# Smaller array tiles for score and pointwise products in a four-layer attention and convolution kernel

## The chip, the cores and the metric

One core of a Trainium2 chip runs the whole kernel. The time is device time in microseconds of one execution; a version is measured in several executions and the median is taken. TensorE multiplies matrices in an array of 128 rows by 128 columns. A product whose contraction has 64 or fewer elements, or whose result has 64 or fewer rows, can be put in a part of the array (a tile), and products in different tiles can run beside one another. A "64x128 tile" here has 64 rows (contraction) and 128 columns (rows of the result). Each f32 product appears in the profile as two matmul instructions, each with its own weight load, so the counts in the profile are twice those in the code.

## The reference

The input is a tensor `x` of 4 images, 64 by 64 positions, 64 channels, f32. Four layers follow one another:

```
layer 0   q, k, v = x Wq + bq, x Wk + bk, x Wv + bv     (per image, 4096 tokens of 64 channels)
          a = softmax(q k^T) over the keys;  out[n] = sum over queries m of a[m, n] v[m];  x = gamma * out + x
layer 1   y = layernorm(x); y = pointwise 64->256; depthwise 3x3; y = y1 * y2
          y = y * channel_weights(mean(y)); x = x + beta * pointwise 128->64 (y)
          z = layernorm(x); z = pointwise 64->256; z = z1 * z2; x = x + gamma * pointwise 128->64 (z)
layer 2   scores between the 64x64 positions of one map (softmax attention over 4096 entries); x = x + result
layer 3   theta, phi, g = x theta_W, x phi_W, x g_W      (64 -> 32 channels)
          y = softmax(theta phi^T) g; wy = y w_W + w_b; wy normalised over the batch; x = x + wy
```

In layer 2 the reference reads the tensor with its axes as (B, C, H, W), so that it too is attention of 4096 entries by 4096, with a contraction of 64. Layers 0, 2 and 3 each hold two large products per image: the scores (4096 x 4096 results) and the products of the exponentials with the values.

## The kernel before

The fast path keeps all four images in SBUF in the tile `X`, channels in partitions: partitions 0 to 63 hold one half of an image's tokens, 64 to 127 the other half. A second, general path runs only if a check of ranges at the end asks for it; it does not run on these inputs, and the change does not touch it.

PSUM is cut into two pools. `new_ps` gives one of three slots `ps` of 128 partitions by 1024 f32 (two banks each, so each half of 512 columns is one bank), `new_acc` one of two slots `acc` of 128 by 512. The exponentials go to six buffers `e` of 128 by 2048 in SBUF.

The order of the work is written out by hand for TensorE, ScalarE and VectorE (`manual_schedule`). `items` is a list of score steps, 32 per image for layers 0 and 2 and 64 per image for layer 3, each with an estimate of its length. `run` walks the list: it issues the score step of item i, lets two lanes (`conv` for layer 1, `misc` for projections, loads and closings) issue what has come due by the estimated clock, then issues what `due[i]` holds, above all the products of an earlier item, and lets the lanes run again. The order is fixed when the program is built and does not depend on measured times. The sequence of layers is: layer 0 of the four images, with layer 1 of each image threaded through layer 0 of the next; layer 2 of image 0, with layer 1 of the last image (and the end of that of image 2) threaded through; then layer 2 of image 1, layer 3 of image 0, layer 2 of image 2, layer 3 of image 1, layer 2 of image 3, layer 3 of images 2 and 3.

The places that matter here:

- Layer 0 scores, L1008: item t computes 128 columns of scores against all 4096 tokens as four `ps` slots (g = 0 to 3). In a slot, r = 0, 1 picks the row half of the array and the bank of the slot; both products use the same 128 columns of `m.q` as weights in 64x128 tiles. ScalarE takes the exponential of each slot (L1012). The products of earlier items, L1032, use the whole 128 rows and 64 columns: 128x64 tiles.
- Query projection, L975: the same form as a score slot, with the weights `wq`, before VectorE adds the bias (L979).
- Layer 1 pointwise products from 64 to 256 channels, L1103 and L1160: per image 8 tiles of `ps` each, 64x128, then a copy by ScalarE (L1108, L1165) or VectorE (L1167).
- Layer 2 scores, L1207, and products, L1224: both in 64x64 tiles already, four to a `ps` slot (`quads`), and not changed.
- Layer 3 scores, L1321: item n takes two `ps` slots at once; four products of contraction 32, one for each group of 32 rows (k = 0 to 3), 32x128 tiles. Slot k // 2, half k % 2. ScalarE then takes the two exponentials (L1326). The products, L1348, are in 128x32 tiles; a sum of the exponentials is made by VectorE (L1344) or, one item in ten, by TensorE (L1337).

A score step starts when its `ps` slot has been read by the exponential that used it last; a product step starts when the exponentials of its item are there.

Of the kernel before, what the change touches and what calls it, by code (L numbers as in the profile page):

```python
# [691 lines left out]
def fast_path(ctx: ExitStack, tc: tile.TileContext, a: dict, out: bass.AP, bad):  # L692
# [36 lines left out]
    mm = nc.tensor.matmul  # L729
# [236 lines left out]
    def project0(b):  # L966
        x, m = X[:, b], im[b]
        m.q, yv = new_big("q"), new_big("yv")
        m.y = yv[:, 0:2048]
        m.v = yv[:, 2048:4096].rearrange("p (t c) -> p t c", c=C)  # L970
        for j, w in ((0, "q"), (0, "v"), (1, "q"), (2, "q"), (1, "v"), (3, "q")):
            ps = new_ps()
            if w == "q":
                for s in range(2):
                    mm(  # L975
                        ps[:, bass.ts(s, 512)], wq[64 * s : 64 * s + 64, :], tok(x, s, j),
                        start=True, stop=True,
                    )
                nc.vector.tensor_scalar_add(  # L979
                    m.q[:, 0:N].rearrange("p (s n) -> p s n", s=2)[:, :, bass.ts(j, 512)],  # L980
                    ps.rearrange("p (s n) -> p s n", s=2), bqk,
                )
            else:
                for i in range(8):
                    mm(ps[:, bass.ts(i, 128)], x[:, bass.ts(8 * j + i, 128)], wv, start=True, stop=True)  # L985
                for s in range(2):
                    nc.vector.tensor_add(
                        m.v[:, 16 * s + 8 * j : 16 * s + 8 * j + 8, :],
                        ps.rearrange("p (t s c) -> p t s c", s=2, c=C)[:, :, s, :],
                        bv.unsqueeze(1).to_broadcast([128, 8, C]),  # L990
                    )
            yield 3.4
# [3 lines left out]
    def layer0(b):  # L996
        x, m, first = X[:, b], im[b], len(items)
        tiles = {}

        def scores(t):  # L1000
            es = [new_e() for _ in range(2)]
            zs = sm.tile([128, 4], F32, tag="zs", name="zs", bufs=4)
            vq = sm.tile([128, C], F32, tag="vq", name="vq", bufs=4)
            for g in range(4):
                ps = new_ps()
                for r in range(2):
                    rows_ = slice(64 * r, 64 * r + 64)
                    mm(  # L1008
                        ps[:, bass.ts(r, 512)], m.q[rows_, bass.ts(t, 128)],
                        x[rows_, bass.ts(g, 512)], start=True, stop=True,  # L1010
                    )
                act(  # L1012
                    es[g // 2][:, bass.ts(g % 2, 1024)], ps, AF.Exp, bias=SHIFT0,
                    accum_out=zs[:, g : g + 1],
                )
            tiles[t] = es, vq, zs

        def scale(t):
            es, vq, zs = tiles[t]
            tot = sums0[:, b, t : t + 1]  # L1020
            nc.vector.tensor_reduce(tot, zs, AX.X, ALU.add)
            rec = sm.tile([128, 1], F32, tag="rec", name="rec")
            nc.vector.reciprocal(rec, tot)
            nc.vector.tensor_scalar_mul(vq, m.v[:, t, :], rec)

        def products(p, half):
            accs = [new_acc() for _ in range(2)]
            for t in (2 * p, 2 * p + 1):
                es, vq, _ = tiles[t]
                for g in range(2):  # L1030
                    for r in range(2):
                        mm(  # L1032
                            accs[g][64 * r : 64 * r + 64, :], vq,
                            es[half][:, 1024 * g + 512 * r : 1024 * g + 512 * r + 512],
                            start=t == 2 * p, stop=t == 2 * p + 1,
                        )
            for g in range(2):
                cols = bass.ts(2 * half + g, 512)
                stt(  # L1039
                    (x if p == 15 else m.y)[:, cols], accs[g], gam0,  # L1040
                    (m.y if p else x)[:, cols], ALU.mult, ALU.add,
                )

        for t in range(32):
            items.append((lambda t=t: scores(t), 3.6))
        for p in range(16):
            for half in range(2):
                at(first + 2 * p + 2 + half, lambda p=p, half=half: products(p, half))
        for t in range(32):
            at(first + t, lambda t=t: scale(t))  # L1050
# [34 lines left out]

    def layer1(b):
        x = X[:, b]
        y = xn.tile([128, 2048], F32, tag="xn", name="xn")
        yield from norm(x, y)
        yg = new_big("yg")[:, 0:N].rearrange("p (w h) -> p w h", h=H)  # L1090
        ysum = sm.tile([128, 4], F32, tag="ysum", name="ysum")
        for r in (1, 0):
            pad = new_pad()
            nc.gpsimd.memset(pad[:, 0:PW], 0.0)
            nc.gpsimd.memset(pad[:, 65 * PW : 66 * PW + 2], 0.0)
            nc.gpsimd.memset(
                pad[:, PW : 65 * PW].rearrange("p (w h) -> p w h", h=PW)[:, :, 0:1], 0.0
            )
            inner = pad[:, PW + 1 : 65 * PW + 1].rearrange("c (p q s h) -> c q p s h", p=2, s=2, h=PW)
            for j in range(4):  # L1100
                ps = new_ps()
                for s in range(2):
                    mm(  # L1103
                        ps[:, bass.ts(s, 512)], pw1[64 * s : 64 * s + 64, bass.ts(r, 128)],
                        tok(y, s, j), start=True, stop=True,
                    )
                for s in range(2):
                    act(  # L1108
                        inner[:, bass.ts(j, 4), :, s, 0:H],
                        ps[:, bass.ts(s, 512)].rearrange("c (q p h) -> c q p h", p=2, h=H),  # L1110
                        AF.Identity, bias=pwb[:, 0, r : r + 1],
                    )
                yield 3.5
            for j in range(4):
                w0 = 16 * j
                y2 = yg[:, w0 : w0 + 16, :]
                out_ = y2 if r else new_t("y1").rearrange("p (w h) -> p w h", h=H)
                for k in range(9):
                    o = (w0 + k % 3) * PW + k // 3
                    win = pad[:, o : o + 16 * PW].rearrange("p (w h) -> p w h", h=PW)[:, :, 0:H]  # L1120
                    wt = V("L1_conv_dw_w", 2 * k + r)
                    if k == 0:
                        nc.vector.tensor_scalar(out_, win, wt, V("L1_conv_dw_b", r), ALU.mult, ALU.add)
                    else:
                        stt(out_, win, wt, out_, ALU.mult, ALU.add)  # L1125
                    yield 1.8
                if not r:
                    stt(y2, out_, 1.0, y2, ALU.mult, ALU.mult, accum_out=ysum[:, j : j + 1])
                    yield 1.8
# [3 lines left out]
        ps = new_ps()  # L1133
# [21 lines left out]
        for j in range(4):  # L1155
            t, u = new_t(), new_t("u")
            for r in range(2):
                ps = new_ps()
                for s in range(2):
                    mm(  # L1160
                        ps[:, bass.ts(s, 512)], pw3[64 * s : 64 * s + 64, bass.ts(r, 128)],
                        tok(z, s, j), start=True, stop=True,
                    )
                if r == 0:
                    act(t, ps, AF.Identity, bias=pwb[:, 1, 0:1])  # L1165
                else:
                    stt(u, ps, pwb[:, 1, 1:2], t, ALU.add, ALU.mult)  # L1167
                yield 3.5
            ps = new_ps()
            for s in range(2):  # L1170
                mm(ps[64 * s : 64 * s + 64, 0:512], pw4, u[:, bass.ts(s, 512)], start=True, stop=True)  # L1171
            act(t[:, 0:512], ps[:, 0:512], AF.Identity, bias=resb[:, 1:2], scale=V("L1_conv_gamma"))
            xs = x[:, bass.ts(j, 512)]
            nc.vector.tensor_add(xs, xs, t[:, 0:512])
            yield 3.5
# [135 lines left out]
    def layer3(b):  # L1311
# [3 lines left out]
        def scores(n):  # L1315
            nb, mc = n // 32, n % 32
            e = es[n] = new_e()
            tiles = [new_ps(), new_ps()]
            for k in range(4):
                rows_ = slice(32 * k, 32 * k + 32)  # L1320
                mm(  # L1321
                    tiles[k // 2][:, bass.ts(k % 2, 512)], m.ph[rows_, bass.ts(mc, 128)],
                    m.th[rows_, bass.ts(nb, 512)], start=True, stop=True,
                )
            for kp in range(2):
                act(e[:, bass.ts(kp, 1024)], tiles[kp], AF.Exp)  # L1326

# [272 lines left out]
```

## Time and profile before

| What | Value |
|---|---|
| Time, median of 3 runs | 2721.74 us (2719.4 to 2723.67) |
| Span of the profiled execution | 2718.6 us |
| Scores of layer 0, L1008, busy | 482.7 us, 2048 matmuls |
| Scores of layer 2, L1207, busy | 470.4 us, 4096 matmuls |
| Scores of layer 3, L1321, busy | 321.2 us, 2048 matmuls |
| Products of layers 0, 2, 3 (L1032, L1224, L1348), busy | 468.4, 468.0 and 272.0 us |
| Pointwise, L1103 and L1160, busy | 35.8 and 35.0 us, 128 matmuls each |
| Query projection, L975, busy | 17.1 us, 64 matmuls |
| Granted TensorE clock, mean | 0.994 |

The profile is of one execution. "PE" is TensorE's matmuls, "PEld" its weight loads, "ACT" ScalarE, "DVE" VectorE. A group is named by its line, then out<-in by tile names, rows*columns of the array, and the shape of the data that streams through it. The chain of waits is followed back from the last instruction; in order of time it lists start, length, engine, tile, line and how many instructions were merged in a piece. The length of a piece in it runs to the start of the next one, so waits inside it are part of it. In the timeline of one engine, what stands in brackets is the idle time before a piece and what ended it.

### The profile page before, as it was taken

Reading aid. Unit: us, or ns where it says so; the run is one execution under the profiler, and the core shown is the slowest. Engines: PE = TensorE matmul, PEld = TensorE weight load, DVE = VectorE, ACT = ScalarE, POOL = GpSimd, SP = SyncE. Lnnn points to the kernel's source line nnn. Section 1 sums busy time; section 2 is a strip of 40 time slices with the busy share of each in tenths; the row PEclk is TensorE's granted clock in tenths of the full one; section 3 lists DMA queues with packets and bytes.
Section 4 is the critical chain, followed back from the end, with each engine's and each line's share of the span. In section 5 each row is a group of like instructions: output and inputs, shape, how many; then the busy total and the mean of one; then the engine's idle time right before and its main releaser. Section 6 shows DMA issues by size and latency. Waiting matters only on the chain.

```text
span 2718.6 us, 41825 instructions
## 1 busy us (share of the span) xinstructions
PE 2656.8 (98%) x18042; PEld 902.6 (33%) x18042; DVE 1349.0 (50%) x1507; ACT 1724.6 (63%) x2796; POOL 16.6 (1%) x66
## 2 busy tenths in 40 slices
PE   8999999999999999999999999999999999999996
PEld 3343333333333333323333332243322333322222
DVE  3232478437773478216720027920058700088888
ACT  4545655565556555555655668855678756578886
POOL 2000000000000000000000000000000000000000
PEclk9999999999999999999999999999999999999998
DMA  3000000000000000000010000010000010010001
GB/s 71 0 1 1 1 1 1 1 1 1 1 1 1 8 8 1 1 1 17 1 32 1 16 1 1 1 32 1 17 1 1 1 32 1 1 32 1 1 1 64
DMA packets 17349, 24.33 MB, mean 9 GB/s; under 512 B 2460, under 2 KB 10885, under 8 KB 17157
## 3 DMA queue, kind: packets, MB, share of 16 engines
q1 hardware_dynamic: 16085, 20.47, 3.1%
q8 instruction: 143, 2.34, 0.4%
q0 software_dynamic: 672, 0.56, 0.1%
q10 hardware_dynamic: 400, 0.56, 0.1%
q14 instruction: 49, 0.40, 0.0%
HBM read 4.80 MB, written 4.19 MB: 3 GB/s over the span
## 4 chain that ended last, share of the span: by engine, by line
PE 94%; DVE 4%; ACT 2%; issue 0%; DMA 0%; ACTq 0%; DVEq 0%
PE acc L1032 17%; PE ps L1008 17%; PE acc L1224 16%; PE ps L1207 16%; PE ps L1321 11%; PE acc L1348 9%; PE ps L1103 1%; PE ps L1160 1%; PE accz L1337 1%; PE ps L1078 1%; PE ps L1143 1%; PE ps L1171 1%; PE ps L1064 1%; PE ps L1302 1%; PE ps L985 1%; DVE tg L1344 0%
## 5 line engine op out<-in xcount | busy, mean ns | idle before, releaser
L1012 ACT ACTIVATE e<-ps 128x1024 f32<-128x1024 f32 x512 | 517.1, 1024 | 343.4 <-PE ps L1008 231.0
L1215 ACT ACTIVATE e<-ps 128x1024 f32<-128x1024 f32 x512 | 517.1, 1024 | 308.1 <-PE ps L1207 308.0
L1326 ACT ACTIVATE e<-ps 128x1024 f32<-128x1024 f32 x512 | 495.4, 1022 | 94.9 <-PE ps L1321 85.1
L1344 DVE TENSOR_TENSOR tg<-tg,e 128x2048 f32<-128x2048 f32 x214 | 490.4, 2292 | 26.1 <-ACT e L1326 7.4
L1008 PE MATMUL ps<-X,q 64*128 64x512 f32 x2048 | 482.7, 608 | 11.3 <-ACT e L1012 4.2
L1207 PE MATMUL ps<-ko 64*64 64x512 f32 x4096 | 470.4, 593 | 7.8 <-ACT ko L1189 5.5
L1224 PE MATMUL acc<-e,X 64*64 64x512 f32 x4096 | 468.0, 591 | 2.7 <-DVE X L1039 2.1
L1032 PE MATMUL acc<-e,vq 128*64 128x512 f32 x2048 | 468.4, 599 | 0.0
L1321 PE MATMUL ps<-tg,ph 32*128 32x512 f32 x2048 | 321.2, 640 | 0.5 <-ACT e L1326 0.5
L1039 DVE SCALAR_TENSOR_TENSOR yv<-acc,gam,yv 128x512 f32<-128x512 f32 x224 | 168.0, 750 | 290.4 <-PE acc L1032 278.6
L1008 PEld LDWEIGHTS ps<-X,q 64*128 64x128 f32 x2048 | 187.0, 187 | 295.3 <-issue 190.1
L1348 PE MATMUL acc<-e,tg 128*32 128x512 f32 x2048 | 272.0, 603 | 1.3 <-ACT yz L1354 1.3
L1207 PEld LDWEIGHTS ps<-ko 64*64 64x64 f32 x4096 | 156.4, 133 | 294.7 <-issue 196.4
L1224 PEld LDWEIGHTS acc<-e,X 64*64 64x64 f32 x4096 | 159.6, 133 | 280.3 <-issue 265.0
L1032 PEld LDWEIGHTS acc<-e,vq 128*64 128x64 f32 x2048 | 136.6, 137 | 311.7 <-issue 290.3
L1232 DVE TENSOR_TENSOR ph<-ph,acc 128x512 f32<-128x512 f32 x16 | 11.0, 688 | 423.7 <-ACT ph L1231 423.7
L1321 PEld LDWEIGHTS ps<-tg,ph 32*128 32x128 f32 x2048 | 103.2, 182 | 219.2 <-issue 139.9
L1125 DVE SCALAR_TENSOR_TENSOR yg<-pad,vec,yg 128x1024 f32<-128x1024 f32 x128 | 164.3, 1283 | 5.9 <-ACT pad L1108 2.4
L1125 DVE SCALAR_TENSOR_TENSOR y<-pad,vec,y 128x1024 f32<-128x1024 f32 x128 | 164.3, 1284 | 3.7
L1348 PEld LDWEIGHTS acc<-e,tg 128*32 128x32 f32 x2048 | 43.5, 108 | 190.6 <-issue 185.1
L1215 ACT ACTIVATION_READ_ACCUMULATOR e<-ps 128x1 f32 x512 | 106.0, 207 | 0.0
L1012 ACT ACTIVATION_READ_ACCUMULATOR e<-ps 128x1 f32 x512 | 106.0, 207 | 0.0
(187 smaller groups left out, 996.5 us busy)
## 6 DMA issues: line engine op xcount, KB each, us to landing
ph<-tg SPq DMA_DIRECT2D x64, 128.0 KB
ko<-ko SPq DMA_DIRECT2D x16, 256.0 KB
out_dram<-o SPq DMA_DIRECT2D x8, 512.0 KB
xr<-in_x_dram SPq DMA_DIRECT2D x14, 256.0 KB
xr<-in_x_dram ACTq DMA_DIRECT2D x2, 256.0 KB
pw<-in_L_conv_pw_w_dram POOLq DMA_DIRECT2D x4, 64.0 KB, 4.6
sca<-in_L_conv_sca_w_dram POOLq DMA_DIRECT2D x1, 64.0 KB, 6.2
pw<-in_L_conv_pw_w_dram POOLq DMA_DIRECT2D x2, 32.0 KB, 4.8
```

The source lines that it names most:

```text
L1008: mm(ps[:, bass.ts(r, 512)], m.q[rows_, bass.ts(t, 128)], x[rows_, bass.ts(g, 512)], start=True, stop=True,)
L1012: act(es[g // 2][:, bass.ts(g % 2, 1024)], ps, AF.Exp, bias=SHIFT0, accum_out=zs[:, g : g + 1],)
L1032: mm(accs[g][64 * r : 64 * r + 64, :], vq, es[half][:, 1024 * g + 512 * r : 1024 * g + 512 * r + 512], start=t == 2 * p, stop=t == 2 * p + 1,)
L1039: stt((x if p == 15 else m.y)[:, cols], accs[g], gam0, (m.y if p else x)[:, cols], ALU.mult, ALU.add,)
L1125: stt(out_, win, wt, out_, ALU.mult, ALU.add)
L1207: mm(ps[64 * c : 64 * c + 64, bass.ts(r, 512)], m.ko[rows_, 128 * jb + 64 * c : 128 * jb + 64 * c + 64], m.ko[rows_, bass.ts(2 * ib + r, 5 ...
L1215: act(es[n, jb], ps, AF.Exp, bias=SHIFT2, accum_out=m.zs[:, jb, ib : ib + 1])
L1224: mm(acc[r][64 * c : 64 * c + 64, :], xw[rows_, jb, :], es[n, jb][rows_, bass.ts(c, 512)], start=jb == 0, stop=jb == 31,)
L1321: mm(tiles[k // 2][:, bass.ts(k % 2, 512)], m.ph[rows_, bass.ts(mc, 128)], m.th[rows_, bass.ts(nb, 512)], start=True, stop=True,)
L1326: act(e[:, bass.ts(kp, 1024)], tiles[kp], AF.Exp)
L1344: nc.vector.tensor_add(esum, esum, e)
L1348: mm(st["y"][32 * k : 32 * k + 32, :], m.gx[:, mc, :], e[:, bass.ts(k, 512)], start=mc == 0, stop=mc == 31,)
```

## The change

The three kinds of product that had contraction 64 or 32 and 128 columns are cut into two of 64 columns. The results land in the same places of the same `ps` slots, and ScalarE and VectorE read them as before. In layer 0 the two row halves and two column halves of a slot become four 64x64 tiles, the form that layer 2 has already; in layer 3 each group of 32 rows has two tiles of 64 columns, eight for an item, and the four tiles of the first slot are issued ahead of the four of the second. The pointwise products of layer 1 go through a helper, `pointwise`, that does the same. It is for a smaller weight load per tile and for fewer different shapes of tile in sequence. The order of all other work stays.

```diff
@@ project0
             if w == "q":
-                for s in range(2):
-                    mm(
-                        ps[:, bass.ts(s, 512)], wq[64 * s : 64 * s + 64, :], tok(x, s, j),
-                        start=True, stop=True,
-                    )
+                for o in range(0, 128, 64):
+                    for s in range(2):
+                        mm(
+                            ps[o : o + 64, bass.ts(s, 512)], wq[64 * s : 64 * s + 64, o : o + 64],
+                            tok(x, s, j), start=True, stop=True,
+                        )
@@ layer0, scores
-                for r in range(2):
-                    rows_ = slice(64 * r, 64 * r + 64)
-                    mm(
-                        ps[:, bass.ts(r, 512)], m.q[rows_, bass.ts(t, 128)],
-                        x[rows_, bass.ts(g, 512)], start=True, stop=True,
-                    )
+                for c in range(2):
+                    for r in range(2):
+                        rows_ = slice(64 * r, 64 * r + 64)
+                        mm(
+                            ps[64 * c : 64 * c + 64, bass.ts(r, 512)],
+                            m.q[rows_, 128 * t + 64 * c : 128 * t + 64 * c + 64],
+                            x[rows_, bass.ts(g, 512)], start=True, stop=True,
+                        )
@@ layer1 (called for pw1 and for pw3, in place of the loop over s with 128 columns)
+        def pointwise(ps, w, r, src, j):
+            for o in range(0, 128, 64):
+                for s in range(2):
+                    mm(
+                        ps[o : o + 64, bass.ts(s, 512)],
+                        w[64 * s : 64 * s + 64, 128 * r + o : 128 * r + o + 64],
+                        tok(src, s, j), start=True, stop=True,
+                    )
@@ layer3, scores
-            for k in range(4):
-                rows_ = slice(32 * k, 32 * k + 32)
-                mm(
-                    tiles[k // 2][:, bass.ts(k % 2, 512)], m.ph[rows_, bass.ts(mc, 128)],
-                    m.th[rows_, bass.ts(nb, 512)], start=True, stop=True,
-                )
+            for kp in range(2):
+                for c in range(2):
+                    for i in range(2):
+                        rows_ = slice(64 * kp + 32 * i, 64 * kp + 32 * i + 32)
+                        mm(
+                            tiles[kp][64 * c : 64 * c + 64, bass.ts(i, 512)],
+                            m.ph[rows_, 128 * mc + 64 * c : 128 * mc + 64 * c + 64],
+                            m.th[rows_, bass.ts(nb, 512)], start=True, stop=True,
+                        )
```

More of the change, by code (lines that the diff above doesn't have):

```diff
@@ L1101, in layer1 @@
                 ps = new_ps()
[L1102 to L1105, printed above, removed]
-                    )
+                pointwise(ps, pw1, r, y, j)
                 for s in range(2):
@@ L1158, in layer1 @@
                 ps = new_ps()
[L1159 to L1163, printed above, removed]
+                pointwise(ps, pw3, r, z, j)
                 if r == 0:
@@ L1318, in scores @@
             tiles = [new_ps(), new_ps()]
-            for k in range(4):
-                rows_ = slice(32 * k, 32 * k + 32)
-                mm(
-                    tiles[k // 2][:, bass.ts(k % 2, 512)], m.ph[rows_, bass.ts(mc, 128)],
-                    m.th[rows_, bass.ts(nb, 512)], start=True, stop=True,
-                )
+            for kp in range(2):
[7 more added lines that the diff above has]
+                        )
             for kp in range(2):
```

## The prediction

> **What bounds the kernel now.** I read the page's busy times and chain first, then the chain in order of time for one stretch of each layer, then the weight loads, alone, over the same stretches.
>
> ```profile
> PE 2656.8 (98%) x18042; PEld 902.6 (33%) x18042; DVE 1349.0 (50%) x1507; ACT 1724.6 (63%) x2796; POOL 16.6 (1%) x66
> PE 94%; DVE 4%; ACT 2%; issue 0%; DMA 0%; ACTq 0%; DVEq 0%
> ```
>
> TensorE is busy 98% of the span and holds 94% of the chain, so time taken off its queue is time off the kernel, unless ScalarE or VectorE is close behind in that stage. No queue is shortened in arithmetic by this change: what it can reach is the seams between blocks of matmuls. The chain in order of time (start, length, line) shows them, first in layer 0, then in layer 2:
>
> ```profile
> 94.31 3.63 PE ps L1008 x16
> 97.94 3.58 PE acc L1032 x16
> 101.53 3.63 PE ps L1008 x16
> ```
>
> ```profile
> 1311.05 3.43 PE acc L1224 x32
> 1314.48 3.43 PE ps L1207 x32
> 1317.91 3.43 PE acc L1224 x32
> ```
>
> Both layers stream eight rounds of 512 columns per block (a round is one pass over all tiles of the array at once; an f32 product takes two). In layer 2, where both products use 64x64 tiles, a block is 3.43 us, 0.429 us a round. In layer 0, where 64x128 scores alternate with 128x64 products, it is 3.63 and 3.58. The surplus, 0.20 and 0.15 us, is paid per change of tile shape. The weight loads split it:
>
> ```profile
> 101.46 0.30 PEld L1008 LDWEIGHTS ps<-X,q 64*128 64x128 f32 x4 [0.81 <-issue]
> 101.99 0.19 PEld L1008 LDWEIGHTS ps<-X,q 64*128 64x128 f32 x2 [0.24 <-issue]
> 102.42 0.19 PEld L1008 LDWEIGHTS ps<-X,q 64*128 64x128 f32 x2 [0.23 <-issue]
> ```
>
> The first round of scores lasts 101.46 to 101.99, 0.53 us, against 0.43 for the next: 0.10 us of first load is exposed. The same reading for a 64x64 block after a change of shape (starts at 1218.04, 1218.52, 1218.95) gives 0.48: 0.05 exposed, because that load has 64 columns. Matmuls on the two sides of any seam start 0.52 us apart in the trace where inside a block it is 0.43: 0.09 us of drain, for every pair of shapes I looked at, 128x64 to 64x64 among them.
>
> **What the Trainium skill says.** "TensorEngine Tiling (Array Packing)", Key Properties, says that a change of tiling mode drains TensorE and that a change of tile inside a mode does not; the 0.52 against 0.43 us agrees. "TensorE: Matmul & The Clock Gate", LDWEIGHTS, says that a load's time goes with its columns, not its rows. The groups agree: 187 ns for 64 rows and 128 columns, 182 for 32 rows and 128 columns, 133 for 64 columns, 108 for 32. Part 3 of that page lets tiles with both rows and columns split run together, at some 4 ns a tile; here their starts are 6.7 ns apart.
>
> **Part 1, layer 0 scores and query projections.** The same products become twice as many instructions with half the columns. Rounds: unchanged, two per ps tile. Seams: L1032 stays at 128x64, so every seam stays, with its 0.09 drain. The exposed load falls from 0.10 to 0.05, and four tiles instead of two start the last one 2 x 6.7 ns later: 3.63 should become 3.59, which is what layer 2 blocks between two seams take (below). There are 135 entries into 64x128 blocks after another shape than 64x64, by the same count of the trace's order as in part 2 (128 score blocks and the projections and pointwise blocks beside them, less those that follow one another without a seam). At 0.04 us each: 5.4 us. The mean from one L1008 block's first load to the next line's is 3.82 against a median of 3.63, so about a quarter wait for ScalarE inside the block and may give nothing back: I take 100 entries, 4.0 us, and keep 5.4 as the other end.
>
> **Part 2, pointwise weights.** L1103 and L1160 have 32 tiles each. Those in layer 0 are in part 1. For the last image (and the end of the third) the work runs between layer 2 blocks:
>
> ```profile
> 1208.73 3.59 PE acc L1224 x32
> 1212.33 1.06 PE ps L1103 x4
> 1213.39 3.67 PE ps L1207 x32
> 1217.05 1.06 PE ps L1103 x4
> ```
>
> At 64x64 all of this has one shape. The tile should fall from 1.06 to two rounds, 0.86, and the neighbour from 3.59 to 3.43: 0.36 us for two seams, 0.18 for one. In the trace's order of matmuls I count 20 seams from 64x64 into a pointwise tile and 18 back (two tiles stand together, others border on L1171, L1237, L1302 or L1078). 38 x 0.18 = 6.8 us. The ps slots and the ScalarE or VectorE work that empties them are unchanged.
>
> **Part 3, layer 3 scores.**
>
> ```profile
> 1643.78 1.07 PE ps L1321 x8
> 1644.85 1.00 PE acc L1348 x8
> 1645.85 1.24 PE ps L1321 x8
> 1647.09 1.00 PE acc L1348 x8
> ```
>
> A block is two rounds (0.86) with 0.10 exposed load, 0.09 drain and 0.02 of staggered starts: 1.07. Every block has a seam on both sides, 256 of them. In every second one the second ps slot is not free yet (it waits for the first exponential of the item before), hence 1.24. With 32x64 tiles the entry falls by 0.05; eight tiles instead of four add 4 x 6.7 ns: 1.07 becomes 1.045. That eight tiles run in one round is seen in the key projection, L1287, of eight 64x32 tiles:
>
> ```profile
> 1394.48 1.02 PE ps L1287 x16
> ```
>
> 0.86 + 0.02 (load of 32 columns) + 0.09 + 0.05 (starts) = 1.02. So a PE-bound block gains 0.028. In a block that waits, the loop is: scores of slot A, exponential, release, scores into A again. Because the edit finishes slot A's four tiles before it touches slot B's, A is ready after its fourth tile: 0.05 less load, two starts more, 0.041 sooner. Gain per item 0.028 to 0.041, times 256: 7.2 to 10.5 us; I take 8.8.
>
> The waits stay where they were: as built, the scores carry 466 waits for ScalarE before and after, on the first tile of a slot. Behind each queue the rest of that slot and the products, and behind those ScalarE's copies. ScalarE has room: in its timeline over the same stretch two exponentials (L1326) take 1.94 us of an item of some 2.15 (L1321 and L1348 above), with gaps of 0.19 to 0.33 us that all end with L1321. VectorE's sum L1344 takes 2.29 us in nine of ten items, 20.6 us in ten, against TensorE's 22.4 (10 x 2.15 and one round trip of accz, 0.86): neither takes over for a gain of 0.04. Row tiles may not meet in a bank of PSUM ("TensorEngine Tiling", PSUM Pressure); each keeps its own half of a ps tile, and no run here shows the other case.
>
> **Sum.** 4.0 + 6.8 + 8.8 = 19.6 us: 2721.7 - 19.6 = 2702.
>
> **The rivals.**
> Seams cheaper, layer 3 not: parts 1 and 2 come, but in layer 3 ScalarE's loop or the eight loads at once eat the gain. For it: the gaps of ScalarE are only 0.2 us. Against: they end with TensorE. 2721.7 - 10.8 = 2711.
> Issue takes over, slower: an item of layer 3 goes from 16.8 pairs of load and matmul to 24.8 (8 in the products, 0.8 in accz). The densest sustained stretch, layer 2, is 32 pairs in 3.43 us, 107 ns a pair, and shows no higher rate over microseconds; at that rate an item takes 2.66 us. Now it is 21% of 2718.6 / 256 = 2.23 (chain shares of L1321, L1348 and L1337), so the worst end is +110 - 11: 2821. The other end is L1287, 16 pairs in 1.02 us, 64 ns, out of a filled queue: nothing lost. Layer 3 breaks even at 2.23 / 24.8 = 90 ns; at 95 the item takes 2.36 us: 0.126 x 256 = +32, -11, 2743. Against it: layer 2 runs at exactly the streaming rate, so 107 is a floor of what the sequencer can do, not a ceiling.
> Cheaper seams than I read: 64x64 and 128x64 share columns; if their seam lost its drain, 128 x 2 x 0.09 = 23 us more, 2679. Against: the trace has 16 such seams, at 0.52 us.
>
> **How the numbers follow.** First case 0.68, layer 3 not 0.14, issue 0.11, cheaper seams 0.03; the rest, 0.04, is no visible change (every shortened seam met by a wait). The range takes in all of part 1 and the upper end of part 3 (5.4 + 6.8 + 10.5 = 22.7: 2699) less 4 for what I can't see, and on the other side the second case and 2 us of spread in the measurement: 2695 to 2713. Faster by over 5.4 us: 0.68 + 0.14 + 0.03 and some of the rest, 0.85; same 0.05; slower 0.10.
>
> **What would show it.** Layer 0 score blocks of 3.59 in the chain with loads of 133 ns; pointwise tiles of 0.86 beside layer 2 blocks of 3.43; layer 3 blocks of 1.045 and every second one 0.04 shorter. Wrong would be: layer 3 blocks over 1.07 with idle TensorE put down to issue, second rounds that start later than 0.48 us after the first, or ScalarE without gaps in layer 3.

## The result and the profile after

The changed kernel takes 2703.18 us in the median (2701.16 to 2704.93, 4 runs) against 2722.56 us before (2719.4 to 2723.67, 4 runs): ratio 0.993, 95% interval 0.9913 to 0.9948, 19.4 us less. The forecast was 2702 us, 19.6 less. That the two agree to 0.2 us is luck: beside the experiments the kernel before took 2719.3 to 2719.6 us, against which 2703.18 is 16 us less, and each of the three terms turns out to be 1 to 2 us off.

The page's busy line and chain first, as before. The counts of matmuls and loads are up by 4416, and TensorE is still the bound:

```profile
PE 2638.6 (98%) x22458; PEld 830.6 (31%) x22458; DVE 1348.6 (50%) x1507; ACT 1724.4 (64%) x2796; POOL 16.7 (1%) x66
PE 93%; DVE 4%; ACT 2%; issue 0%; DMA 0%; ACTq 0%; DVEq 0%
```

The chain in order of time, in undisturbed layer 0: the score block has gone from 3.63 to 3.60, the product block stays at 3.58.

```profile
96.43 3.60 PE ps L1010 x32
100.02 3.58 PE acc L1035 x16
103.60 3.60 PE ps L1010 x32
```

The weight loads say why. The first round now takes 96.36 to 96.84, 0.48 us, where it took 0.53; the next ones are 0.43 as ever:

```profile
96.36 0.21 PEld L1010 LDWEIGHTS ps<-X,q 64*64 64x64 f32 x8 [0.81 <-issue]
96.84 0.15 PEld L1010 LDWEIGHTS ps<-X,q 64*64 64x64 f32 x4 [0.28 <-issue]
97.27 0.15 PEld L1010 LDWEIGHTS ps<-X,q 64*64 64x64 f32 x4 [0.28 <-issue]
```

The chain where pointwise tiles (now L1095) stand between layer 2 blocks:

```profile
1202.33 3.43 PE acc L1229 x32
1205.77 0.86 PE ps L1095 x8
1206.62 3.68 PE ps L1212 x32
1210.31 1.00 PE ps L1095 x8
1211.31 3.43 PE acc L1229 x32
```

Beside products L1229 the seams are gone: 0.86 and 3.43. Beside scores L1212 they are gone too, but the block takes 3.68 and the tile after it 1.00: something else fills the time. And layer 3:

```profile
1633.59 1.04 PE ps L1328 x16
1634.63 1.00 PE acc L1356 x8
1635.63 1.21 PE ps L1328 x16
1636.84 1.00 PE acc L1356 x8
```

1.07 became 1.04, and every second one, 1.24, became 1.21. Elsewhere the blocks alternate between 1.13 and 1.18, and these became 1.10 and 1.15.

To see where the time went I cut each execution at the first score load of each layer (the trace gives its start): "layer 0" runs from its first score to the first score of layer 2, "layer 2, images 0 and 1" to the first score of layer 3, "layer 3" is the sum of its three phases, the last one to the end. Layer 2 of images 2 and 3 stays at 465.3 to 465.5 us in all runs and is left out.

One thing has to be taken off first. In every trace the granted TensorE clock is at half for stretches of 3.41 us or two to four of them in a row, and some of them fall in other places from run to run. Here is one score block whose code is the same in two runs. The first line is the chain of the kernel before, the last one that of p3_layer3_only. Between them stands the stretch of the kernel before in which the clock is low: start and end, length, busy time of PE, PEld, DVE, ACT and POOL, the clock as a share of full speed (0.51), DMA.

```profile
803.05 5.33 PE ps L1008 x16
803.10:806.50 3.40, 3.40 (x10) 1.38 (x12) 0.69 (x1) 1.89 (x3) 0.00 (x0) 0.51 0.00 0
804.60 3.63 PE ps L1008 x16
```

5.33 against 3.63: a stretch costs 1.7 us, half its length. In the table, layers 0 and 2 have this cost already taken off; how much it was stands in brackets. In layer 3 the clock falls only after the last products, and nothing is taken off.

| Run | Layer 0 | Layer 2, images 0 and 1 | Layer 3 | Time, median |
|---|---|---|---|---|
| before | 1047.0 (6.8) | 537.7 (3.4) | 644.2 | 2722.56 |
| changed | 1041.3 (5.1) | 532.4 (5.1) | 636.6 | 2703.18 |
| p1_scores_only | 1045.5 (3.4) | 538.2 (5.1) | 644.0 | 2717.67 |
| p2_pointwise_only | 1050.1 (1.7) | 532.3 (5.1) | 645.1 | 2715.51 |
| p12_no_layer3 | 1041.2 (5.1) | 532.3 (5.1) | 643.6 | 2709.25 |
| p3_layer3_only | 1047.0 (5.1) | 538.5 (3.4) | 638.2 | 2711.07 |
| l3_columns_outer | 1040.6 (6.8) | 532.3 (3.4) | 658.6 | 2722.98 |
| l3_tiles_32x32 | 1041.4 (5.1) | 532.3 (3.4) | 642.7 | 2708.00 |
| relief_before | 1044.4 (5.1) | 538.0 (5.1) | 644.3 | 2717.76 |
| relief_scores_only | 1044.8 (5.1) | 538.0 (5.1) | 644.0 | 2717.64 |
| relief_pointwise_only | 1048.2 (6.8) | 531.6 (3.4) | 644.1 | 2714.57 |
| relief_changed | 1039.1 (5.1) | 531.7 (3.4) | 636.8 | 2695.92 |
| relief_all_pads | 1043.5 (3.4) | 532.0 (3.4) | 637.8 | 2701.52 |

The phases are of one execution each. Where two kernels have the same code in a phase of layer 0 or 2, they agree to 0.8 us with the clock taken off. The kernel before, run again beside the experiments, had medians of 2719.26 to 2719.61. So the change gives 5.7 us in layer 0, 5.3 in layer 2 and 7.6 in layer 3.

TensorE's blocks follow one another in the same order in all runs, so they can also be matched one by one, from a block's first matmul to that of the next. The next table adds up the differences at the pointwise tiles with the block on each side of them, where no stretch of half clock lies, and over the rest of layer 0 (half clock taken off). The first row, where the code is the same, shows the noise; the rest of layer 0 is unchanged with pointwise alone too, so there it is up to 0.7 us.

| Run against | Pointwise places, layer 0 | Rest of layer 0 | Pointwise places, layer 2 |
|---|---|---|---|
| p3_layer3_only, before | -0.04 | +0.1 | +0.01 |
| p1_scores_only, before | +2.74 | -4.1 | 0.00 |
| p2_pointwise_only, before | +2.49 | +0.7 | -5.41 |
| p12_no_layer3, before | -1.44 | -4.3 | -5.41 |
| changed, before | -1.45 | -4.2 | -5.41 |
| relief_before, before | -2.60 | +0.1 | -0.15 |
| relief_scores_only, relief_before | +4.68 | -4.3 | 0.00 |
| relief_pointwise_only, relief_before | +4.24 | -0.5 | -6.02 |
| relief_changed, relief_before | -1.37 | -4.0 | -6.03 |

### The profile page after: what moved, and what is told of

It reads as the page before. It is cut to its first block, busy times and chain, and to the rows that moved or that the text cites. A ratio compares the mean times of both kernels' runs of the same rounds, so it can differ in the third digit from the quotient of the medians.

```text
span 2701.4 us, 50657 instructions
## 1 busy us (share of the span) xinstructions
PE 2638.6 (98%) x22458; PEld 830.6 (31%) x22458; DVE 1348.6 (50%) x1507; ACT 1724.4 (64%) x2796; POOL 16.7 (1%) x66
## 4 chain that ended last, share of the span: by engine, by line
PE 93%; DVE 4%; ACT 2%; issue 0%; DMA 0%; ACTq 0%; DVEq 0%
PE acc L1035 17%; PE ps L1010 17%; PE acc L1229 16%; PE ps L1212 16%; PE ps L1328 10%; PE acc L1356 9%; PE ps L1095 2%; PE accz L1345 1%; DVE tg L1352 1%; PE ps L1081 1%; PE ps L1152 1%; PE ps L1176 1%; PE ps L1067 1%; PE ps L1307 1%; PE ps L986 1%; ACT e L1334 0%
## 5 line engine op out<-in xcount | busy, mean ns | idle before, releaser
L1010 PE MATMUL ps<-X,q 64*64 64x512 f32 x4096 | 477.2, 600 | 11.7 <-ACT e L1015 4.4
L1212 PE MATMUL ps<-ko 64*64 64x512 f32 x4096 | 470.6, 593 | 7.8 <-ACT ko L1194 5.5
L1229 PE MATMUL acc<-e,X 64*64 64x512 f32 x4096 | 469.3, 593 | 2.7 <-DVE X L1042 2.1
L1328 PE MATMUL ps<-tg,ph 32*64 32x512 f32 x4096 | 313.6, 613 | 0.5 <-ACT e L1334 0.5
L1042 DVE SCALAR_TENSOR_TENSOR yv<-acc,gam,yv 128x512 f32<-128x512 f32 x224 | 167.9, 750 | 286.1 <-PE acc L1035 275.1
L1229 PEld LDWEIGHTS acc<-e,X 64*64 64x64 f32 x4096 | 161.3, 133 | 279.6 <-issue 264.3
L1212 PEld LDWEIGHTS ps<-ko 64*64 64x64 f32 x4096 | 156.8, 133 | 294.1 <-issue 193.4
L1010 PEld LDWEIGHTS ps<-X,q 64*64 64x64 f32 x4096 | 142.8, 133 | 329.5 <-issue 217.6
L1328 PEld LDWEIGHTS ps<-tg,ph 32*64 32x64 f32 x4096 | 79.8, 129 | 221.4 <-issue 139.9
```

What stands on the lines that cost most here:

```text
L1010: mm(ps[64 * c : 64 * c + 64, bass.ts(r, 512)], m.q[rows_, 128 * t + 64 * c : 128 * t + 64 * c + 64], x[rows_, bass.ts(g, 512)], start=Tru ...
L1042: stt((x if p == 15 else m.y)[:, cols], accs[g], gam0, (m.y if p else x)[:, cols], ALU.mult, ALU.add,)
L1212: mm(ps[64 * c : 64 * c + 64, bass.ts(r, 512)], m.ko[rows_, 128 * jb + 64 * c : 128 * jb + 64 * c + 64], m.ko[rows_, bass.ts(2 * ib + r, 5 ...
L1229: mm(acc[r][64 * c : 64 * c + 64, :], xw[rows_, jb, :], es[n, jb][rows_, bass.ts(c, 512)], start=jb == 0, stop=jb == 31,)
L1328: mm(tiles[kp][64 * c : 64 * c + 64, bass.ts(i, 512)], m.ph[rows_, 128 * mc + 64 * c : 128 * mc + 64 * c + 64], m.th[rows_, bass.ts(nb, 51 ...
```

## The experiments

**Which part gives what.** Four kernels, each with some of the change's hunks:

```diff
 p1_scores_only:     hunks project0 and layer0          (pointwise and layer 3 as before)
 p2_pointwise_only:  hunk layer1                        (scores and layer 3 as before)
 p12_no_layer3:      hunks project0, layer0 and layer1
 p3_layer3_only:     hunk layer3
```

> Layer 0 scores and the query projection in 64x64 tiles, everything else as before (pointwise still 64x128, layer 3 still 32x128). Seam theory: 115 entries from another shape get 0.04 us cheaper, three quarters of them felt: -3.5 us. But each of the 40 pointwise tiles that lie in layer 0 borders on a score block on one side, which had its shape and now hasn't: a new seam of 0.09 us drain plus 0.05 or 0.10 us of load, 0.17 on average, +6.9 us. Sum about +3 us: 2725 us, ratio 1.001. Rival theory (only the smaller load counts, neighbours don't): -4 to -5 us, 2718, ratio 0.998.

> Only the wide pointwise products in 64x64 tiles. Seam theory: in layer 2, 38 seams go, -6.8 us; in layer 0 the 40 pointwise tiles get a new seam against the 64x128 scores, 40 x 0.15 = +6 us: about -1 us, 2721.5, ratio 1.000. Rival theory (only the smaller load counts): 64 tiles x 0.04 = -2.5 us and nothing else; additive with the scores alone.

> Scores of layer 0, query projection and pointwise in 64x64 tiles; layer 3 scores still 32x128. Seam theory: -4.6 to -5.4 us in layer 0 and -6.8 us in layer 2, some -11 us, 2711 to 2712, ratio 0.996: much more than the sum of the two taken alone (+3 - 1). Rival theory (loads alone): -6.5 us, the sum of the two.

> Only layer 3 scores in 32x64 tiles. Seam theory: 0.028 to 0.041 us an item, 256 items: -7.2 to -10.5 us, 2713 to 2715, ratio 0.997. Rival theory (ScalarE bounds layer 3): 0 us, 2722.

Measured, as ratios to before: scores alone 0.9994 (0.9986 to 1.0003), no difference that shows; pointwise alone 0.9988 (0.9982 to 0.9995); both 0.9962 (0.9948 to 0.9976); layer 3 alone 0.9971 (0.9959 to 0.9982). Layer 3 came as forecast, -8.2 us. Of the other two I had expected +3 and -1 us alone and -11 together. Together they gave -10.0; alone they gave -1.6 and -3.8, so both forecasts for a part alone missed. The parts aren't additive, as the seams have it: at the pointwise places of layer 0 each alone loses 2.5 to 2.7 us, and both together win 1.4. But a loss of 6 to 7 was forecast there for 40 new seams. So a new seam cost 0.06 to 0.07 us on average and not 0.15: either it is cheaper, or something hides it.

The trace of scores alone shows one such place of layer 0. This is the chain before, a pointwise tile on each side of a score block and of one shape with it, the first with a seam ahead of it:

```profile
309.48 1.06 PE ps L1103 x4
310.53 3.70 PE ps L1008 x16
314.24 1.00 PE ps L1103 x4
```

And the chain of p1_scores_only, where both sides of the score block are new seams:

```profile
309.10 1.06 PE ps L1094 x4
310.15 3.66 PE ps L1010 x32
313.82 1.06 PE ps L1094 x4
```

The sums are 5.76 and 5.78: two seams more for 0.02 us. Before, 3.70 was no pure block either: seamless neighbours should have left it at 3.43 and the tile after it at 0.95 (two rounds and the drain at its end). What it waited for is in the timeline of the weight loads before:

```profile
312.11 0.30 PEld L1008 LDWEIGHTS ps<-X,q 64*128 64x128 f32 x4 [0.69 <-ACT pad L1108]
313.11 0.30 PEld L1008 LDWEIGHTS ps<-X,q 64*128 64x128 f32 x4 [0.70 <-ACT e L1012]
314.11 0.30 PEld L1103 LDWEIGHTS ps<-xn,pw 64*128 64x128 f32 x4 [0.70 <-ACT e L1012]
```

A pointwise tile next to a score block makes five or six slots of `ps` in a row. TensorE fills one in 0.86 us, ScalarE empties one in 1.0 us, or in 1.4 if it is a pointwise tile (two copies of 0.70 into `pad`), and there are three slots. From the fourth on, loads come every 1.00 us, each released by ScalarE. Where that is so, a seam that falls into this stretch costs nothing as long as it fits into the wait, and a seam taken out of it gives nothing. In these stretches ScalarE is the bound, in a kernel whose TensorE is busy 98%.

**Is it the slots?** I moved part of ScalarE's copies beside the pointwise tiles to VectorE, in four kernels: the one before, scores alone, pointwise alone, and the changed one.

```diff
                 for s in range(2):
-                    act(inner[..., s, 0:H], ps[:, bass.ts(s, 512)]..., AF.Identity, bias=pwb[:, 0, r : r + 1])
+                    if s == 0:
+                        act(inner[..., s, 0:H], ps[:, bass.ts(s, 512)]..., AF.Identity, bias=pwb[:, 0, r : r + 1])
+                    else:
+                        nc.vector.tensor_scalar_add(inner[..., s, 0:H], ps[:, bass.ts(s, 512)]..., pwb[:, 0, r : r + 1])
...
                 if r == 0:
-                    act(t, ps, AF.Identity, bias=pwb[:, 1, 0:1])
+                    nc.vector.tensor_scalar_add(t, ps, pwb[:, 1, 0:1])
```

> The kernel before, with part of the copies behind the pointwise tiles moved from ScalarE to VectorE: one of the two copies into pad (0.70 us each), and the first of the two copies of the second pointwise product (1.12 us). Nothing else changes; seams as before. Slot theory: beside a pointwise tile five or six ps slots are filled in a row, and the last ones wait for ScalarE (0.2 to 0.5 us in about 25 places); this frees them sooner: -3 to -5 us, 2715 to 2717. Rival (the waits there are not slots, or VectorE is as late): 0, 2720.

> Scores and query projection alone in 64x64 tiles (pointwise 64x128), with the same copies moved to VectorE. Slot theory: the new seams beside the pointwise tiles, which a slot wait hid without the move, now cost 20 to 40 x 0.15 us; the gain against the kernel before with the same move falls from 1.6 us to nothing or turns to a loss of up to 3 us: 2716 to 2719. Rival: the difference stays at -1.6 us.

> Pointwise alone in 64x64 tiles, with the same copies moved to VectorE. Slot theory: in layer 0 the new seams now cost some 3 to 6 us, in layer 2 the 38 seams taken away give their 6.8 us instead of 3.7: against the kernel before with the same move -1 to -4 us, 2712 to 2715, with layer 2 shorter by 6 to 7 us and layer 0 longer. Rival: layer 2 keeps 3.7.

> The changed kernel with the same copies moved to VectorE. Slot theory: no new seams here, and the seams taken away in layer 2 give their full 6.8 us: 19 to 22 us under the kernel before with the same move, 2695 to 2698, and so 4 to 7 us under the changed kernel. Rival (slots don't matter): 2702 to 2703.

Ratios: 0.9992 (0.9984 to 1.0001), 0.9991 (0.9985 to 0.9998), 0.998 (0.9971 to 0.9989) and 0.9911 (0.9898 to 0.9925). The first is a miss: the move alone gains 1.8 us by the medians (2.6 at the pointwise places of layer 0), not 3 to 5. The question was what it does to the seams, and the second table answers it. At the pointwise places of layer 0 the new seams now cost 4.68 us (scores alone) and 4.24 (pointwise alone), where they cost 2.74 and 2.49: 0.11 to 0.12 us each. In layer 2 the seams taken away give 6.0 us, where they gave 5.4. The three forecasts for times with the move came true: against relief_before -0.1, -3.2 and -21.8 us. But the waits are worth less than I had thought, in layer 2 0.6 us and not 3. The same place of layer 0, first relief_before, then relief_scores_only:

```profile
311.21 1.06 PE ps L1103 x4
312.27 3.57 PE ps L1008 x16
315.84 0.86 PE ps L1103 x4
```

```profile
309.36 1.06 PE ps L1094 x4
310.42 3.59 PE ps L1010 x32
314.01 1.06 PE ps L1094 x4
```

5.49 and 5.71: with the slots freed sooner, the new seams cost 0.22 us here instead of 0.02. And relief_changed, which has one seam ahead of the first tile and none after:

```profile
309.13 1.02 PE ps L1095 x8
310.14 3.54 PE ps L1010 x32
313.69 0.86 PE ps L1095 x8
```

5.42. So the slot wait hid part of the cost of the new seams. Not all of what is missing from the forecast comes out: two seams were priced at 0.33 us (0.09 of drain each, 0.05 and 0.10 of load) and cost 0.22 here. The score block of relief_before is still 3.57 long where nothing in its way would leave 3.43, so a wait is left there; how much it hides is not shown. relief_changed is also 7.3 us faster than the changed kernel by medians from different sets of runs (their ratio intervals, 0.9898 to 0.9925 and 0.9913 to 0.9948, overlap at the edge), and the fastest kernel of this study. 3.0 of the 7.3 us lie between the medians of the kernel before in the same two sets, and in the traces its pointwise places are 2.5 and 0.8 us shorter, so the gain may be nearer to 3 or 4 us.

**All of the copies?** In relief_changed VectorE's copy of a tile still waited for ScalarE's copy into the same `pad`, so the two ran one after the other.

```diff
-                    if s == 0: act(...)
-                    else: nc.vector.tensor_scalar_add(...)
+                    nc.vector.tensor_scalar_add(...)
```

> The changed kernel with both copies into pad and the first copy of the second pointwise product on VectorE. In the run with one of the two pad copies moved, that copy waited for ScalarE's (32 times, 74.8 us in all), and score loads still waited 9.3 us in 12 places for it. Slot theory: without ScalarE in these slots the release comes sooner and ScalarE's exponentials are 0.7 us a tile sooner too: 1 to 4 us under that run's 2695.9, 2692 to 2695. Rival (VectorE's own queue, with 1.5 us of L1042 ahead of the copy, holds the slot just as long): 2696, or up to 2 us more.

Measured 2701.52, ratio 0.9938 (0.9924 to 0.9952): 5.6 us worse than with one copy moved. The rival of that expectation held, and more strongly than it said. The chain of relief_all_pads at this place runs through VectorE:

```profile
304.03 3.61 PE acc L1035 x16
307.63 0.03 issue
307.66 0.75 DVE yv L1042
308.41 0.07 DVE sums L1024
...
308.71 0.26 DVE vq L1027
308.96 0.67 DVE pad L1119
309.63 0.03 issue
309.66 0.76 DVE pad L1119
310.42 0.14 issue
310.56 1.95 PE ps L1010 x16
```

The copy stands in VectorE's queue behind the evacuation of the products that ended just before (L1042) and the scaling of the next weights. It starts 1.3 us after those products' end and holds its slot to 310.42. With the copies split, the chain at this place has nothing but TensorE in it (the three lines of relief_changed above).

**The order of the slots.**

```diff
-            for kp in range(2):
-                for c in range(2):
+            for c in range(2):
+                for kp in range(2):
                     for i in range(2):
```

> The changed kernel with the two outer loops of the layer 3 scores exchanged: first the left column half of both slots, then the right half of both. Same tiles, same seams. Theory (slot order matters): in the items whose second slot is not free at the start (every second one, 0.17 us), the first slot's right half now stands behind that wait, so its exponential starts up to 0.17 us later and hands the delay to the next release: up to 128 x 0.17 = +22 us on the changed kernel's 2703, 2710 to 2725, with block L1328 longer than 1.21 us in every second item. Rival (tiles of other columns start on their own, order is free): 2703, within 1 us.

2722.98 us, ratio to before 1.0014 (1.0007 to 1.002): some 20 us slower than the changed kernel, all of it in layer 3 (658.6 us against 636.6), and a little slower than the kernel with no change at all. The chain:

```profile
1641.62 1.24 PE ps L1328 x16
1642.85 1.00 PE acc L1356 x8
1643.85 1.24 PE ps L1328 x16
1645.08 1.00 PE acc L1356 x8
```

I had expected the long block in every second item; it is in nearly every one (35 of 256 stay at 1.04), which fits a late exponential that hands its delay to the next item. ScalarE's timeline shows the other half: before each item's pair of exponentials it now idles 0.29 us for L1328 (0.16 to 0.27 in the changed kernel):

```profile
1642.90 1.94 ACT L1334 ACTIVATE e<-ps 128x1024 f32<-128x1024 f32 x2 [0.29 <-PE ps L1328]
1645.13 1.94 ACT L1334 ACTIVATE e<-ps 128x1024 f32<-128x1024 f32 x2 [0.29 <-PE ps L1328]
```

The tiles are the same ones; "slot by slot" is what lets them gain.

**Smaller still.** Layer 3 scores in 32x32 tiles:

```diff
-                for c in range(2):
+                for c in range(4):
...
-                            tiles[kp][64 * c : 64 * c + 64, bass.ts(i, 512)],
-                            m.ph[rows_, 128 * mc + 64 * c : 128 * mc + 64 * c + 64],
+                            tiles[kp][32 * c : 32 * c + 32, bass.ts(i, 512)],
+                            m.ph[rows_, 128 * mc + 32 * c : 128 * mc + 32 * c + 32],
```

> The changed kernel with layer 3 scores in 32x32 tiles: 16 tiles and 32 pairs of load and matmul for an item, 40.8 pairs with its products. Seam theory: 0.025 less exposed load than with 64 columns, 8 starts of 6.7 ns more: a TensorE-bound block goes from 1.044 to 1.07, one that waits stays as it is: +4 to +7 us on 2703, so 2707 to 2710. Rival (issue has a ceiling near the densest rate seen before, 64 ns a pair): an item takes 40.8 x 64 = 2.61 us against 2.2, +100 us, some 2800.

2708.00, ratio to before 0.9958 (0.9945 to 0.9972): 5 us more than the changed kernel, within the forecast from staggered starts, and nothing like a ceiling of issue.

```profile
1635.36 1.21 PE ps L1328 x32
1636.57 1.00 PE acc L1356 x8
1637.56 1.09 PE ps L1328 x32
1638.65 1.00 PE acc L1356 x8
```

32 pairs of load and matmul went through in 1.09 us, 34 ns a pair, and 80 pairs in these 4.3 us, 54 ns a pair. The shorter block is 1.09 us long where 1.07 was forecast and the changed kernel has 1.04, which fits eight starts more of 7 ns each against a smaller load, if not in full.

## Why the prediction was right

- **Seams, not arithmetic.** Right. Rounds stay at 0.43 us; what moved is the first round of a block (0.53 to 0.48) and the number of seams. That neighbours count is shown by relief_pointwise_only: the same tiles lose 4.2 us in layer 0 and win 6.0 in layer 2.
- **Part 1, 4.0 us.** Mis-sized: layer 0 fell by 5.7 us, 0.5 of it in a product at the start of the run that p3_layer3_only has shorter too, so 5.2. The price of an entry was right: the score block goes from 3.634 to 3.594 us in the median. The count of 100 entries was too low. Of the 102 score blocks that don't stand beside a pointwise tile, 92 gave 3.6 us together; the 10 of them that were over 3.66 us gave nothing, as "may give nothing back" said. But a quarter was too many to take off: 34 of the 128 blocks are over 3.66 us from their first load to the next line's, and 19 of these stand beside a pointwise tile. The pointwise places gave 1.4 us and the query projections 0.2, and the sum is close to the other end, 5.4.
- **Part 2, 6.8 us.** Mis-sized, 5.4 measured at the pointwise places. "The ps slots and the ScalarE or VectorE work that empties them are unchanged" was true, but unchanged they were the bound beside some of the score blocks. The line 3.67 in my own fence, where a block between two seams should have been 3.59, was the hint. With the slots relieved the term is 6.0; what becomes of the other 0.8 us isn't settled (a recount of the trace finds 19 and 18 seams, which explains 0.2).
- **Part 3, 8.8 us.** 7.6 in the phases, 8.2 by the medians for that part alone, inside its range of 7.2 to 10.5. 1.045 was 1.04. In the trace the 128 shorter blocks gained 0.026 us each and the 128 that wait 0.034, where 0.028 and 0.041 were forecast.
- **The sum.** 4.0 + 6.8 + 8.8 = 19.6 against 5.7 + 5.3 + 7.6 = 18.6 in the phases and 16 to 19.4 by the medians: part 1 was too small by 1 to 2 us and parts 2 and 3 too large by as much each. That they nearly cancel is luck. The joint figure of parts 1 and 2, -10.8 forecast, came out at -10.0 by the medians of p12_no_layer3.
- **The rivals.** ScalarE as the bound of layer 3: refuted, its gaps still end with L1328. Issue: refuted by 54 ns a pair held over items, well under the break-even of 90. Cheaper seams: not seen where nothing waits, 128x64 to 64x64 stands at 0.52 us between starts after the change too, in the median of 127 places.

Not tried: products of layer 0 in 64x64 tiles with the row halves exchanging accumulators, meant to take the last seams out of layer 0. No run here shows whether that can be done.

## What to carry to other kernels

Count the changes of tile shape in the order of TensorE's queue, not only the work in each block: here each cost 0.09 us of drain and, for loads of 64 and 128 columns, 0.05 to 0.10 us of exposed load, and an edit to one product can add or remove them at its neighbours. Before a seam or a load is priced, look at the weight loads after it: where the next ones are released by the engine that empties PSUM, part of the saving turns into a longer wait, and moving half of that engine's work there brought some of it out. Before the phases of two executions are compared, look at the granted clock: a stretch of 3.41 us at half clock costs 1.7 us, as much as many of the differences here. When a step writes several slots, finish one before the next may wait.

## What the runs showed that I had not expected

TensorE took load and matmul pairs at 34 ns each for 1.09 us and at 54 ns over several items, twice the densest sustained rate of the kernel before (107 ns), with 0% of the chain put down to issue. Two new changes of tile shape cost 0.02 us together in a place where a slot wait of ScalarE's covered them. And TensorE's granted clock fell to half for 3.4 to 13.7 us between the first score of layer 0 and the first of layer 2 in every trace, by the brackets in the table, in part at other places each time; what sets it off isn't settled here.
